# Layer 1 of a two-layer kernel: the third image's angle products placed ahead of the second-half result products of the first image

## The chip, the core and the metric

The kernel runs on one core of a Trainium2 chip. The metric is the device time of one execution in microseconds (us). The kernel before takes 1414.39 us, the median of three runs (1414.35 to 1415.5).

## The reference, cut to what matters

The input is x, 16 images of 128 channels and 64 x 64 places. Layer 0 adds to x a diagonal LSTM over its group-normalised values. Layer 1 adds to that result, again group-normalised, a small quantum circuit at every place; it alone concerns us here.

```python
def L1(x, pre_w, pre_b, q_weights, post_w, post_b):
    xf = x.transpose(0, 2, 3, 1).reshape(-1, C)
    xq = xf @ pre_w.T + pre_b            # four angles for each place
    z = _simulate(xq, q_weights)         # sixteen amplitudes, squared, summed with signs
    out = z @ post_w.T + post_b
    return out.reshape(N, H, W, -1).transpose(0, 3, 1, 2)
...
x = x + L0(_gn(x), ...)
x = x + L1(_gn(x), ...)
```

The kernel writes the product of the starting state as sines of sums of angles, so that an image goes through four steps: angle products, sines, amplitude products with their squares, and result products, to which the bias and the input are added.

## The kernel before, in words

Layer 0 takes most of the time (to about 1283 us) and ends with the statistics of layer 1's normalisation. At its end most of x lies in SBUF: rows 24 to 63 of all images in the tile `ring`, and rows 0 to 23 in DRAM (`low`), from where they come back in pieces of 512 columns.

Layer 1 works image by image, on 8 pieces of 512 columns each: pieces 0 to 2 are the reloaded rows, pieces 3 to 7 lie in `ring`. Images are counted from 0, so the third image is image 2. The helpers are:

- `load(n)` (L948) takes up to n free places and issues as many loads of reloaded rows on GpSimd's queue (L954, the DMA itself at L860).
- `angles(b, c)` (L972) makes eight products (L977) for image b into one PSUM bank, `theta`: four column strips of 32, each the sum of two products. With c = 0 or 1 it takes one half of 256 columns of each piece; without c, all 512. Pool `ps_t` has one bank.
- `sines(b, c)` (L987) is a generator. Its first part reads `theta` on ScalarE (L992, y), rounds on VectorE (L994, near) and subtracts (L995). Its second part, at the next call, is the sine on ScalarE (L997).
- `squares(b, c)` (L999) makes two products of 64 rows each (L1006, am, two banks) and squares them on ScalarE (L1019).
- `outputs(b, h, c)` (L1021) makes four products of 32 rows each (L1028, po) for one half h of the pieces, into four banks of the pool `ps_o`, which has five.
- `finish(b, h, po, c)` (L1038) adds bias and x to each on VectorE (L1053), which frees its bank, and issues the output's DMA on SyncE's queue (L1054). For the reloaded pieces it also gives their places back to `load`.

Each product is recorded as two matmuls. The order is written out by hand (`tc.manual_schedule()`, L1065): each engine executes its instructions in the order of the calls, and the framework only adds the waits. The first image goes in halves of 256 columns, so that work starts early; then image 1 and the rest go whole. From image 1 on, a loop (L1100) repeats: outputs(b, 0), first part of sines(b + 2), finish, load, squares(b + 1), second part of the sines, outputs(b, 1), finish, load, angles(b + 3). Ahead of the loop this pipeline is filled by hand, and there the change lies (L1086 to L1099).

Of the kernel before, what the change touches and what calls it, by code (L numbers as in the profile page):

```python
# [80 lines left out]
def kernel(  # L81
# [866 lines left out]
    def load(n):  # L948

        while n and places and len(lows) < NT * NB:  # L950
            v = places.pop(0)
            lows.append(v)
            if len(lows) > 8:
                low_rows(nc.gpsimd, len(lows) - 1, v)  # L954
            n -= 1

    def rows_of(b, k):
        if k < NT:
            return lows[NT * b + k]
        q = block(2 * ROWS * k)  # L960
        return ring[:, q : q + 2, b, :]

    def half(v, c):

        if c is None:
            return v
        return v[:, c] if len(v.shape) == 3 else v[:, c * BLOCK : (c + 1) * BLOCK]

    def bank(pool, name):
        return pool.tile([P, CHUNK], F32, name=name, tag=pool.name)  # L970

    def angles(b, c=None, all_of=None):  # L972
        th = half(bank(ps_t, f"theta{b}_{c}") if all_of is None else all_of, c)
        for h in range(2):

            for j in (2, 3, 1, 0):
                nc.tensor.matmul(  # L977
                    th[32 * j : 32 * j + 32, :],
                    lhsT=w_image[:, b, 16 - 16 * h : 48 - 16 * h],
                    rhs=half(rows_of(b, 2 * j + h), c),  # L980
                    start=(h == 0),
                    stop=(h == 1),
                    tile_position=(0, 32 * j),
                )
        ths[b, c] = th

    def sines(b, c=None):  # L987

        if b not in turns:
            turns[b] = sinp.tile([P, CHUNK], F32, name=f"y{b}", tag="y")  # L990
        y = half(turns[b], c)
        nc.scalar.activation(y, ths[b, c], AF.Identity, bias=b_image[:, b : b + 1])  # L992
        near = half(nearp.tile([P, CHUNK], F32, name=f"near{b}_{c}", tag="near"), c)
        nc.vector.tensor_scalar(near, y, ROUND, ROUND, ALU.add, ALU.subtract)  # L994
        nc.vector.tensor_sub(y, y, near)  # L995
        yield
        nc.scalar.activation(y, y, AF.Sin, scale=TWO_PI)  # L997

    def squares(b, c=None):  # L999
        ams = []  # L1000
        y = half(turns[b], c)
        for h in range(2):
            am = half(ps_a.tile([P, CHUNK], F32, name=f"am{b}_{h}_{c}", tag=f"am{h}"), c)

            k = 64 * h
            nc.tensor.matmul(  # L1006
                am,
                lhsT=w_amp[k : k + 64, h, :],
                rhs=y[k : k + 64, :],
                start=True,  # L1010
                stop=True,
                tile_position=(k, 0),
            )
            ams.append(am)

        if b not in sqs:
            sqs[b] = [sqp.tile([P, CHUNK], F32, name=f"sq{b}", tag="sq"), turns[b]]
        for am, v in zip(ams, sqs[b]):
            nc.scalar.activation(half(v, c), am, AF.Square)  # L1019

    def outputs(b, h, c=None):  # L1021
        po = [
            half(bank(ps_o, f"po{b}_{h}_{j}_{c}"), c)
            for j in range(4)
        ]
        for j in range(4):
            k = 32 * j
            nc.tensor.matmul(  # L1028
                po[j],
                lhsT=w_out[k : k + 32, :],  # L1030
                rhs=half(sqs[b][h], c)[k : k + 32, :],
                start=True,
                stop=True,
                tile_position=(k, 0),
            )
        return po

    def finish(b, h, po, c=None):  # L1038
        for j in range(4):
            k = 4 * h + j  # L1040
            v = rows_of(b, k)
            x1, y, o = half(v, c), po[j], ov[b, :, k * CHUNK : (k + 1) * CHUNK]
            to = place = v
            if c is not None:
                o, to = o[:, c * BLOCK : (c + 1) * BLOCK], x1
            elif k >= NT:


                q = block(2 * ROWS * k)
                to = ring[:, q, b - 1 : b + 1, :] if b % 2 else ring[:, q + 1, b - 2 : b, :]  # L1050
                y = y.rearrange("p (k n) -> p k n", n=BLOCK)
                place = to.rearrange("p k n -> p (k n)")
            nc.vector.scalar_tensor_tensor(to, y, b_out, x1, ALU.add, ALU.add)  # L1053
            nc.sync.dma_start(out=o, in_=to if c is not None else place)  # L1054
            if c is None or c == 1 and k < NT:
                places.append(place)

    def idle():

        ps = bank(ps_t, nc.get_next_instruction_name())  # L1060
        v = w_image.rearrange("p b k -> p (b k)")[:, 0:CHUNK]
        for _ in range(2):
            nc.tensor.matmul(ps, lhsT=w_out, rhs=v, start=True, stop=True)  # L1063

    with tc.manual_schedule():  # L1065
        load(len(places))

        angles(0, 0)
        angles(0, 1, bank(ps_o, "theta0"))
        first = [sines(0, c) for c in range(2)]  # L1070
        for later in first:
            next(later)

        th = bank(ps_t, "theta1")
        angles(1, 0, th)
        for later in first:
            next(later, None)
        squares(0, 0)
        angles(1, 1, th)
        ths[1, None] = th  # L1080
        po = outputs(0, 0, 0)
        finish(0, 0, po, 0)
        squares(0, 1)
        later = sines(1)
        next(later)
        po = outputs(0, 1, 0)  # L1086
        finish(0, 1, po, 0)
        next(later, None)
        po = outputs(0, 0, 1)
        finish(0, 0, po, 1)  # L1090
        load(3)
        angles(2)
        later = sines(2)
        next(later)
        po = outputs(0, 1, 1)
        squares(1)
        next(later, None)
        finish(0, 1, po, 1)
        angles(3)  # L1099
        for b in range(1, NB):  # L1100
            po = outputs(b, 0)
            later = sines(b + 2) if b + 2 < NB else iter(())
            finish(b, 0, po)
            load(3)
            next(later, None)
            if b + 1 < NB:
                squares(b + 1)
            next(later, None)
            po = outputs(b, 1)
            finish(b, 1, po)  # L1110
            load(3)
            if b + 3 < NB:
                angles(b + 3)
            elif b < NB - 1:
                idle()
# [37 lines left out]
```

## Time and profile before

| | |
|---|---|
| median of three runs | 1414.39 us |
| profiled execution | 1416.6 us |
| its span | 1414.8 us |
| start of layer 1's first angle products | 1288.34 us |
| first output DMA issued | 1294.66 us |
| last result on VectorE | 1401.2 us |
| TensorE busy | 1351.9 us (96%) |
| VectorE busy | 981.1 us (69%) |
| ScalarE busy | 778.4 us (55%) |
| GpSimd busy | 921.3 us (65%) |

The profile is that of one execution. Its times are in us from the start of the span. A row of the timeline gives the start, the length, the engine, the line and the operation with its output, inputs and shapes; xN says that N like instructions are merged. What stands in brackets is the idle time of the engine just ahead, and what ended it. PE is TensorE, DVE is VectorE, ACT is ScalarE, POOL is GpSimd and SPq is SyncE's DMA queue. [...] A row of the table of stretches gives the stretch, then the busy time of each engine in it, the granted share of TensorE's clock, the mean busy share of the 16 DMA engines, and what they moved in GB/s. A share over 1 comes of packets that overlap.

### The profile page before, as it was taken

To read this page: it belongs to the slowest core of one execution; us is meant where nothing else is said; L and a number is where in the kernel's file an instruction comes from. 1 tells how busy PE (TensorE), PEld (TensorE's weight loads), DVE (VectorE), ACT (ScalarE), POOL (GpSimd) and SP (SyncE) were. 2 spreads that over 40 slices of the span, in tenths; PEclk is the share of its full clock that TensorE was granted. 3 is DMA by queue.
4 is the path that set the end of the run, shared out by engine and by line. 5 is a ranking of instruction groups with operands and counts; after the bars stand their busy time and mean duration, and the time that the engine had idled before them with its cause. 6 is when DMAs were issued, how large, how long until landed. Compare 5 with 4: busy or idle time off the path is not lost. (4 is left out here: it accounts for less than half of the span.)

```text
span 1414.8 us, 20302 instructions
## 1 busy us (share of the span) xinstructions
PE 1351.9 (96%) x6030; PEld 960.6 (68%) x6030; DVE 981.1 (69%) x2549; ACT 778.4 (55%) x1860; POOL 921.3 (65%) x1823
## 2 busy tenths in 40 slices
PE   6778999999999999999999999999999999989995
PEld 5658887777776667667777767677777778785331
DVE  7983565566665666787777776666665567866995
ACT  4555666555555555555555555555555566554331
POOL 4226787777776667788888876777777667762300
PEclk9999999999999999999999999999999999999998
DMA  9980000000000000133333100000000000004999
GB/s 327 368 282 2 1 2 0 1 1 1 1 0 1 0 1 1 60 119 120 119 120 120 60 1 1 0 1 1 1 1 0 1 1 1 9 24 157 371 399 353
DMA packets 78926, 107.06 MB, mean 76 GB/s; under 512 B 5552, under 2 KB 53712, under 8 KB 78816
## 3 DMA queue, kind: packets, MB, share of 16 engines
q1 hardware_dynamic: 74176, 94.39, 19.1%
q0 software_dynamic: 3408, 10.58, 2.1%
q8 instruction: 48, 0.79, 0.2%
q10 hardware_dynamic: 1232, 0.80, 0.2%
q14 instruction: 62, 0.51, 0.1%
HBM read 59.61 MB, written 46.14 MB: 75 GB/s over the span
## 5 line engine op out<-in xcount | busy, mean ns | idle before, releaser
L583 PE MATMUL ps<-spare,wxT 128*128 128x512 f32 (+18 forms) x1280 | 479.7, 518 | 0.7 <-POOL spare L574 0.7
L767 DVE TENSOR_TENSOR ps<-ps,both 128x256 f32<-128x256 f32 (+9 forms) x544 | 221.7, 408 | 304.9 <-PE ps L752 303.4
L771 ACT ACTIVATE ps<-ps,bias 128x512 f32<-128x512 f32 (+23 forms) x480 | 279.3, 583 | 220.2 <-DVE ps L767 183.7
L752 PE MATMUL ps<-spare,w1T 128*128 128x256 f32 (+16 forms) x1272 | 345.8, 353 | 9.8 <-DVE spare L834 4.9
L583 PEld LDWEIGHTS ps<-spare,wxT 128*128 128x128 f32 x1280 | 230.9, 190 | 173.2 <-issue 155.5
L752 PE MATMUL ps<-spare,w0T 128*128 128x256 f32 (+16 forms) x1272 | 343.8, 352 | 0.8 <-POOL spare L608 0.8
L802 ACT COPY both<-ps 128x256 f32<-128x256 f32 (+9 forms) x544 | 191.6, 355 | 180.8 <-PE ps L752 161.2
L617 POOL TENSOR_TENSOR ring<-ring,spare 128x256 f32<-128x256 f32 (+8 forms) x487 | 247.7, 541 | 31.2 <-DVE stats L705 21.1
L752 PEld LDWEIGHTS ps<-spare,w1T 128*128 128x128 f32 x1272 | 229.8, 190 | 35.7 <-DVE spare L834 7.6
L752 PEld LDWEIGHTS ps<-spare,wsT 128*128 128x128 f32 x1088 | 194.9, 190 | 86.4 <-DVE spare L834 34.7
L752 PE MATMUL ps<-spare,wsT 128*128 128x256 f32 (+14 forms) x1088 | 241.3, 365 | 5.4 <-DVE spare L834 3.6
L752 PEld LDWEIGHTS ps<-spare,w0T 128*128 128x128 f32 x1272 | 230.3, 190 | 22.1 <-POOL spare L608 0.9
L574 POOL TENSOR_TENSOR spare<-spare,rstd 128x512 f32<-128x512 f32 (+10 forms) x160 | 171.1, 1069 | 14.8 <-DVE rstd L153 2.3
L569 POOL TENSOR_TENSOR spare<-ring 128x256 f32<-128x256 f32 (+8 forms) x213 | 147.6, 703 | 0.0
L828 ACT ACTIVATE g<-cst 128x256 f32<-128x256 f32 (+20 forms) x320 | 103.0, 368 | 64.4 <-DVE cst L827 63.8
L564 POOL TENSOR_TENSOR spare<-ring,mean 128x16 f32<-128x16 f32 (+8 forms) x247 | 131.2, 541 | 7.4 <-DVE mean L143 7.2
L834 DVE TENSOR_TENSOR spare<-g,ps 128x256 f32<-128x256 f32 (+17 forms) x319 | 105.4, 368 | 43.9 <-ACT g L828 42.0
L608 POOL TENSOR_TENSOR spare<-spare 128x240 f32<-128x240 f32 (+9 forms) x136 | 102.7, 755 | 29.6 <-DVE spare L834 25.7
L771 ACT ACTIVATE g<-ps,bias 128x512 f32<-128x512 f32 (+20 forms) x160 | 97.4, 609 | 27.1 <-DVE ps L767 21.1
L827 DVE TENSOR_TENSOR cst<-cst,ps 128x256 f32<-128x256 f32 (+20 forms) x320 | 104.5, 368 | 5.5
L854 POOL COPY spare<-spare 128x16 f32<-128x16 f32 x64 | 21.1, 330 | 133.8 <-DVE spare L834 133.8
L824 DVE TENSOR_TENSOR ps<-ps,g 128x512 f32<-128x512 f32 (+20 forms) x160 | 95.1, 594 | 17.0 <-ACT g L771 16.6
(368 smaller groups left out, 1096.6 us busy)
## 6 DMA issues: line engine op xcount, KB each, us to landing
out_dram<-ring SPq DMA_DIRECT2D x94, 256.0 KB, 5.1
ring<-in_x_dram SPq DMA_DIRECT2D x80, 256.0 KB, 5.6
low<-ring SPq DMA_DIRECT2D x6, 2048.0 KB, 7.5
ring<-in_x_dram SPq DMA_DIRECT2D x6, 2048.0 KB, 8.1
spare<-in_x_dram SPq DMA_DIRECT2D x27, 256.0 KB, 5.5
rest<-in_x_dram SPq DMA_DIRECT2D x21, 256.0 KB, 5.6
ring<-low POOLq DMA_DIRECT2D x19, 256.0 KB, 6.3
out_dram<-spare SPq DMA_DIRECT2D x14, 256.0 KB, 6.5
```

The lines of the kernel that those rows point to most:

```text
L564: nc.gpsimd.tensor_sub(by_pairs(xn, 0, j, n), x0, over(mean1, n))
L569: nc.gpsimd.tensor_sub(by_pairs(xn, 1, j, n), lower, of)
L574: nc.gpsimd.tensor_mul(v, v, r)
L583: nc.tensor.matmul(ps[g][:, :, a:b], lhsT=wxT[:, g * 128 : (g + 1) * 128], rhs=xns[t % 2][:, :, a:b], start=t > 0, stop=True, skip_group_c ...
L617: engine.tensor_add(x1, x1, by_pairs(new, q, j, n))
L752: nc.tensor.matmul(out, lhsT=w[:, g * 128 : (g + 1) * 128], rhs=rhs, start=False, stop=True, skip_group_check=True,)
L767: nc.vector.tensor_add(v, v, both[g][:, a:b])
L771: nc.scalar.activation(to[:, :, a:w], ps[g][:, :, a:w], FUNC[g], bias=bias[:, g : g + 1])
L802: nc.scalar.copy(both[g][:, a:b], ps[g][:, 0, a:b])
L827: nc.vector.tensor_add(c[:, q], c[:, q], ig[:, q])
L828: nc.scalar.activation(th[:, q, a:w], c[:, q], AF.Tanh)
L834: nc.vector.tensor_mul(new[:, q, a:v], th[:, q, a:v], act[GO][:, q, a:v])
```

## The change

The call angles(2) moves up by three calls. It stood behind outputs(0, 0, 1), its finish and load(3); it now stands ahead of all three, right behind the second part of image 1's sines.

```diff
         po = outputs(0, 1, 0)
         finish(0, 1, po, 0)
         next(later, None)
+        angles(2)
         po = outputs(0, 0, 1)
         finish(0, 0, po, 1)
         load(3)
-        angles(2)
         later = sines(2)
         next(later)
         po = outputs(0, 1, 1)
```

In the built program only TensorE's order differs: the eight products of L977 for image 2 stand ahead of the four of L1028 for outputs(0, 0, 1). The instructions of VectorE, ScalarE, GpSimd and SyncE stand in the same order as before.

## The prediction

> **What bounds the kernel now.** I read the page first, then the chain of waits, then the timeline of layer 1 around the edit, then the busy time by stretch. The chain runs through TensorE products for nearly all of layer 1, but it names the engine that the others wait beside, so I looked at VectorE (DVE) in the timeline. Columns: start, length, engine and line, operation.
>
> ```profile
> 1296.06 0.43 DVE L994 TENSOR_SCALAR near_None<-y 128x512 f32<-128x512 f32 x1 [0.25 <-ACT y L992]
> 1297.12 1.65 DVE L1053 SCALAR_TENSOR_TENSOR ring<-po,b_out,ring 128x256 f32<-128x256 f32 x4
> 1298.69 1.26 DVE L1053 SCALAR_TENSOR_TENSOR spare<-po,b_out,spare 128x256 f32<-128x256 f32 x3
> 1299.87 0.48 DVE L1053 SCALAR_TENSOR_TENSOR ring<-po,b_out,ring 128x256 f32<-128x256 f32 x1
> 1303.48 0.43 DVE L994 TENSOR_SCALAR near_None<-y 128x512 f32<-128x512 f32 x1 [3.13 <-ACT y L992]
> 1304.55 1.65 DVE L1053 SCALAR_TENSOR_TENSOR ring<-po,b_out,ring 128x256 f32<-128x256 f32 x4
> 1307.33 2.07 DVE L1053 SCALAR_TENSOR_TENSOR spare<-po_None,b_out,spare 128x512 f32<-128x512 f32 x3 [1.13 <-PE po_None L1028]
> ```
>
> DVE is idle 3.13 us from 1300.35 to 1303.48, because ScalarE had no angles of the third image (image 2) to read, and 1.13 us before 1307.33. After that it has no gap: in the stretch table below it is busy 82.83 of 84 us. So the two idle times at the start of layer 1 are what can be won. TensorE and ScalarE in the same stretch:
>
> ```profile
> 1295.33 0.69 ACT L992 ACTIVATE y<-theta,b_image 128x512 f32<-128x512 f32 x1
> 1295.95 0.67 PE L1028 MATMUL po<-sq,w_out 32*128 32x256 f32 x2
> 1297.66 1.48 PE L1028 MATMUL po<-sq,w_out 32*128 32x256 f32 x6 [1.04 <-DVE ring L1053]
> 1299.07 1.03 PE L977 MATMUL theta_None<-ring,w_image 128*32 128x512 f32 x2
> 1302.61 0.71 PE L1028 MATMUL po<-y,w_out 32*128 32x256 f32 x8
> 1303.26 1.13 PE L1006 MATMUL am_None<-y,w_amp 64*128 64x512 f32 x4
> 1306.17 1.14 PE L1028 MATMUL po_None<-sq,w_out 32*128 32x512 f32 x8
> ```
>
> The second-half products outputs(0,0,1) start at 1295.95 with one free bank, stand 1.04 us, and then follow DVE bank by bank (1297.66 to 1299.07). Image 2's angles come behind them: 1299.07 to 1302.61 is 3.54 us, where image 3's take 1.85 (1304.32 to 1306.17). The clock column tells why. Columns by stretch: sum, PE, PEld, DVE, ACT, POOL busy, PEclk, DMA share, GB/s.
>
> ```profile
> 1299.00:1300.00 1.00, 1.00 (x9) 0.30 (x12) 1.00 (x4) 0.00 (x0) 0.00 (x0) 0.58 0.81 268
> 1300.00:1301.00 1.00, 1.00 (x12) 0.31 (x8) 0.35 (x1) 0.00 (x0) 0.00 (x0) 0.50 0.77 264
> 1301.00:1302.00 1.00, 1.00 (x8) 0.00 (x0) 0.00 (x0) 0.00 (x0) 0.21 (x1) 0.50 0.75 262
> 1302.00:1303.00 1.00, 1.00 (x12) 0.31 (x8) 0.00 (x0) 0.24 (x1) 0.99 (x3) 0.72 0.34 114
> ```
>
> The granted clock is half for (0.42+0.50+0.50+0.28)/0.5 = 3.4 us, 1299.15 to 1302.55, right behind the thin stretch of TensorE. The end itself belongs to the DMA engines:
>
> ```profile
> 1296.00:1317.00 21.00, 19.96 (x113) 6.42 (x116) 16.55 (x32) 7.12 (x13) 4.30 (x8) 0.92 0.73 239
> 1317.00:1401.00 84.00, 82.10 (x440) 26.68 (x432) 82.83 (x131) 28.14 (x47) 13.97 (x26) 1.00 1.03 396
> 1401.00:1413.00 12.00, 0.00 (x0) 0.00 (x0) 0.22 (x1) 0.00 (x0) 0.00 (x0) 0.52 0.93 351
> ```
>
> From 1317 they are full (share 1.03), and they drain for 11 to 12 us after DVE's last result at 1401.2. Before 1317 they are at 0.73, so 0.27 x 21 = 5.7 us of them lie idle. A shift in layer 1 reaches the end only by taking DMA idle time out of that stretch.
>
> [...]outputs(0,0,1) restarts at 1297.66, 0.06 us after DVE read a bank (1297.12 + 0.48). [...]
>
> **The change, part by part.** One call moves: on TensorE the eight angle products of image 2 (16 records) go ahead of the four of outputs(0,0,1). Nothing is added or removed. DVE, ACT, POOL and SP keep their orders; load(3) keeps its place in POOL's queue, and no DMA is moved.
>
> - *The new start of angles(2).* Its bank is the single theta bank, free when ScalarE has read image 1's angles: 1295.33 + 0.69 = 1296.02. So it starts at about 1296.1, where before one product of outputs(0,0,1) ran. Behind this wait stand outputs(0,0,1), which could start one product 0.1 us earlier; nobody takes that product before 1298.69. The rows of image 2 were loaded long before: the DMA engines are empty from 1292.3 to 1295. At full clock it takes 1.85, to 1297.95.
> - *outputs(0,0,1).* Its banks come free at 1295.81, 1297.60, 1297.99 and 1298.38. From 1297.95 it runs at the same pace as now, and DVE, occupied until 1298.77, takes it from 1298.69 or 1298.75 on as now. Price 0 to 0.1 us, hidden by DVE's own queue; without that cover it would be 1.85.
> - *outputs(0,1,1)* loses its cover. Now it finds all banks free and takes 0.65 as a set. Then it needs the banks that DVE frees from outputs(0,0,1); the last but one comes at 1299.48 + 0.48 = 1299.96. The fourth product starts at 1300.02 and takes 0.63 alone (as 1298.44 to 1299.07 now), to 1300.65. Without this wait it could end at about 1299.7: the new wait costs 0.95, inside the gain.
> - *squares(1)* then starts at 1300.65 instead of 1303.26: **2.61 us earlier**. Its inputs (sine of image 1, 1297.24 + 0.63 = 1297.87) are there. angles(3) follows 1.06 later at 1301.7 and outputs(1,0) at 1303.56; DVE takes the first full-width result at 1307.33 - 2.61 = 1304.72. Image 2's sines run meanwhile: ScalarE reads the angles at 1298.1, DVE rounds at 1300.35 instead of 1303.48 and finishes outputs(0,1,1) at 1303.1. So one idle of 1.6 us remains, instead of 3.13 and 1.13: 4.26 - 1.65 = 2.61 again.
> - *The clock.* The 2.61 holds 1.7 from the dip (3.4 us at half) and 0.9 of order alone: without the dip now, angles(2) would end 1.7 earlier. That the dip goes is an estimate[...]. If it stays, squares(1) and angles(3) pay about 1.3.
> - *Through the DMA engines.* Outputs from outputs(0,1,1) on are issued 2.6 earlier, into a stretch at 0.73. Only the three loads at 1301.79 stay; they land 3.0 us after issue, so by about 1306, ahead of angles(4) at 1310.51 - 2.6 = 1307.9. I take off 0.1 for their meeting the earlier outputs (0 to 0.5). Full DMA then begins near 1314.4 and ends 2.5 earlier.
>
> Sum: -2.6 + 0.1 = -2.5 against the profiled execution (span 1414.8, 1416.6 in all, 1.8 around the span), giving 1412.3 and 1414.1. The median shown is 2.2 below the profiled execution; I carry the difference over: 1414.39 - 2.5 = **1411.9**.
>
> **Rivals.**
> - *No dip in ordinary runs*[...]: only the 0.9 of order is won: 1413.5. For it: the median is 2.2 below the profiled run.[...]
> - *The dip stays or moves onto squares(1) and angles(3)*: 2.6 - 1.3 = 1.3: 1413.1.
> - *DMA-bound whatever is done*: the tail of 12 us swallows the shift, 1414.4. Against: 5.7 us of DMA idle lie ahead of 1317.
> - *Slower, by a dip that the change makes.* Between 1297.95 and 1300.65 TensorE would have only products of 32 rows paced by DVE. [...]half clock falls on angles(3) and outputs(1,0), which nothing covers: +1.7. It decides where the run before had no dip: -0.9 + 1.7 = +0.8: 1415.2.
> - *More than the sum*: were TensorE ready when DVE is, at 1303.1, all 4.26 us of idle would go; with half of the rest, or longer dips now, 3.5: 1410.9.
>
> **How the numbers follow.** Forecast 0.52 (its own range 1411.2 to 1412.6), no dip 0.14, dip stays 0.09, hidden in DMA 0.06, slower 0.08, more 0.11. 0.2% is 2.8 us, about what a measurement can tell from no change, and the bound of faster is 1411.6. Faster: 0.11 and a fifth of the forecast, 0.22. Slower by that much: half of the slower case, 0.04. The rest, 0.74, is within 0.2%. The range 1411.0 to 1413.8 leaves out hidden, slower and half of more, 0.2.
>
> **What would show it.** Right: the theta products of image 2 at 1296.1 taking 1.85; no half clock near 1300; DVE's idle of 3.13 gone and one of about 1.6 before outputs(1,0); DMA full by 1314. Wrong: outputs(0,0,1) later than 1298.8 at DVE, half clock at 1301 to 1305, or a DVE end at 1398.6 with the DMA end still at 1413.

## The result and the profile after

The changed kernel takes 1412.94 us (median of 21 runs, 1412.08 to 1415.7) and the kernel before 1415.5 (21 runs, 1413.18 to 1417.05): 2.56 us less, a ratio of 0.9982 with a 95% interval of 0.9976 to 0.9988. In us the interval is about 1.7 to 3.4. The profiled execution took 1412.49, its span 1410.7. Two later comparisons gave 0.9979 (0.9970 to 0.9989) and 0.9979 (0.9971 to 0.9987), 3.2 and 2.8 us less. The median of three runs that stands ahead of the prediction, 1414.39, was 1.1 us under that of the 21 runs.

VectorE in the timeline of the changed kernel. Layer 1 starts 0.36 us earlier in this execution (first result of `finish` at 1293.78 instead of 1294.14), so 0.36 is to be added to each time before it is laid beside those of the kernel before.

```profile
1295.69 0.43 DVE L994 TENSOR_SCALAR near_None<-y 128x512 f32<-128x512 f32 x1 [0.25 <-ACT y L992]
1296.76 1.65 DVE L1053 SCALAR_TENSOR_TENSOR ring<-po,b_out,ring 128x256 f32<-128x256 f32 x4
1298.33 1.26 DVE L1053 SCALAR_TENSOR_TENSOR spare<-po,b_out,spare 128x256 f32<-128x256 f32 x3
1299.51 0.48 DVE L1053 SCALAR_TENSOR_TENSOR ring<-po,b_out,ring 128x256 f32<-128x256 f32 x1
1299.90 0.42 DVE L994 TENSOR_SCALAR near_None<-y 128x512 f32<-128x512 f32 x1
1300.96 1.65 DVE L1053 SCALAR_TENSOR_TENSOR ring<-po,b_out,ring 128x256 f32<-128x256 f32 x4
1304.34 2.07 DVE L1053 SCALAR_TENSOR_TENSOR spare<-po_None,b_out,spare 128x512 f32<-128x512 f32 x3 [1.73 <-PE po_None L1028]
```

The rounding of image 2 follows the last result without a wait; the idle time of 3.13 us is gone. The one ahead of the full-width results has grown from 1.13 to 1.73. Counted from the first `finish`, VectorE reaches those results at 1304.34 - 1293.78 = 10.56 us, where it was 1307.33 - 1294.14 = 13.19: 2.63 earlier. TensorE and ScalarE:

```profile
1294.97 0.69 ACT L992 ACTIVATE y<-theta,b_image 128x512 f32<-128x512 f32 x1
1295.72 0.62 PE L977 MATMUL theta_None<-ring,w_image 128*32 128x512 f32 x2
1297.58 1.20 PE L1028 MATMUL po<-sq,w_out 32*128 32x256 f32 x8
1298.47 1.87 PE L1028 MATMUL po<-y,w_out 32*128 32x256 f32 x8
1300.27 1.13 PE L1006 MATMUL am_None<-y,w_amp 64*128 64x512 f32 x4
1303.18 1.14 PE L1028 MATMUL po_None<-sq,w_out 32*128 32x512 f32 x8
```

The angles start as soon as ScalarE has left the theta bank (1294.97 + 0.69 = 1295.66) and take 1.86 us. outputs(0,1,1) now takes 1.87 as a set, bank by bank behind VectorE, where it took 0.71. Matmuls of one set overlap: those of the angles start at 1295.72 and 1296.18 and are 0.62 and 0.60 long. The stretch that ran at half clock before:

```profile
1299.00:1300.00 1.00, 1.00 (x7) 0.74 (x6) 1.00 (x4) 0.00 (x0) 0.00 (x0) 1.00 0.80 264
1300.00:1301.00 1.00, 1.00 (x6) 0.30 (x4) 0.97 (x3) 0.00 (x0) 0.00 (x0) 1.00 0.76 266
1301.00:1302.00 1.00, 1.00 (x10) 0.29 (x12) 1.00 (x4) 0.57 (x2) 0.56 (x2) 1.00 0.76 260
1302.00:1303.00 1.00, 1.00 (x12) 0.13 (x4) 0.61 (x2) 1.00 (x3) 0.99 (x2) 1.00 0.74 155
```

The clock column reads 1.00 throughout. TensorE's busy time is 1.00 in each of these rows, as it was in the kernel before at a clock of 0.50 to 0.72: a busy TensorE is not one at its peak. And the DMA engines (last two columns):

```profile
1296.00:1317.00 21.00, 20.86 (x128) 7.04 (x124) 19.13 (x36) 7.72 (x13) 5.89 (x11) 1.00 0.85 289
1317.00:1401.00 84.00, 80.19 (x424) 26.22 (x424) 80.20 (x127) 27.51 (x46) 12.57 (x23) 0.99 1.04 400
1401.00:1413.00 12.00, 0.00 (x0) 0.00 (x0) 0.00 (x0) 0.00 (x0) 0.00 (x0) 0.51 0.58 221
```

Ahead of 1317 their share rose from 0.73 to 0.85, so 0.12 x 21 = 2.5 us of their idle time is gone there, and less is left for the last stretch (0.58 x 12 = 7.0 us of work where it was 0.93 x 12 = 11.2). One thing was not foreseen. TensorE in the timeline at angles(5), and VectorE behind it:

```profile
1313.84 1.05 PE L977 MATMUL theta_None<-ring,w_image 128*32 128x512 f32 x4
1315.03 0.62 PE L977 MATMUL theta_None<-spare,w_image 128*32 128x512 f32 x2
...
1318.03 2.07 DVE L1053 SCALAR_TENSOR_TENSOR low<-po_None,b_out,low 128x512 f32<-128x512 f32 x3 [0.94 <-PE po_None L1028]
```

The angles of image 5 wait for their third reloaded piece, 1.04 us in the timeline (DMA spare<-low), and VectorE stands 0.94 us. Of the 2.63 that VectorE won, it gives this back in this profile. The second profile of the changed kernel, described below, has no such wait, and its layer 1 is no shorter.

### The profile page after: what moved, and what is told of

The parts are those of the page before. It is cut to its first block, busy times and chain, and to the rows that moved or that the text cites. A ratio compares the mean times of both kernels' runs of the same rounds, so it can differ in the third digit from the quotient of the medians.

```text
span 1410.7 us, 20301 instructions
## 1 busy us (share of the span) xinstructions
PE 1352.7 (96%) x6030; PEld 962.4 (68%) x6030; DVE 980.5 (70%) x2549; ACT 778.7 (55%) x1860; POOL 921.3 (65%) x1823
```

## The experiments

The theory: the gain is made of 1.7 us of half clock and 0.9 of order at VectorE, and it reaches the end because it takes idle time from the DMA engines. Rivals: the order alone, the clock alone, VectorE rather than the DMA engines at the end. Since the first result of `finish` stands anywhere from 1293.50 to 1295.54 in profiles with the same layer 0, the table counts layer 1 by itself: from the first result of `finish` (L1053) to the first full-width one, and to the end of the span. A difference of 0.4 there is within what three profiles of one kernel show. The time is the median of the runs of that kernel, and the ratio is to the kernel before in the same comparison, whose median was 1415.5 to 1416.35.

| kernel | time | ratio, 95% | to first full-width result | to the end |
|---|---|---|---|---|
| before (two profiles) | 1415.5, again 1415.86 | | 13.19, 13.16 | 120.7, 119.8 |
| changed (three profiles) | 1412.94, 1413.09, 1413.10 | 0.9982, 0.9979, 0.9979 | 10.56, 10.56, 10.57 | 116.9, 117.0, 117.3 |
| before, with filler | 1414.26 | 0.9989 (0.9983 to 0.9996) | 11.49 | 118.1 |
| changed, squares(1) moved | 1412.42 | 0.9974 (0.9965 to 0.9984) | 9.63 | 117.4 |
| changed, no output of image 8 | 1408.03 | 0.9942 (0.9927 to 0.9958) | 10.56 | 112.0 |
| one step further | 1416.59 | 1.0003 (0.9994 to 1.0011) | 15.29 | 121.8 |
| one step further, with filler | 1414.87 | 0.9992 (0.9986 to 0.9999) | 12.24 | 118.8 |
| changed, seven places, first placing | 1414.95 | 0.9989 (0.9983 to 0.9996) | 10.56 | 116.7 |
| changed, seven places, own pool | 1414.78 | 0.9992 (0.9986 to 0.9999) | 10.56 | 116.3 |
| squares(1) moved and seven places | 1413.86 | 0.9986 (0.9979 to 0.9994) | 9.64 | 115.4 |

**The changed kernel again, and the kernel before again.**

> The changed kernel once more, to have it beside the others on one chip. Theory (order and clock): about 2.5 us under the median of the kernel before, with the granted clock of nearly all runs at 0.995 or 0.996; the runs of the kernel before fall into two groups, one near 1413.6 at the higher clock and one near 1416.6 at the lower. Rival (order alone): the groups of the kernel before are noise and have nothing to do with the clock.

1413.09 (10 runs) beside 1416.27 (34 runs). The granted clock of the changed kernel's runs was 0.994 to 0.996, that of the kernel before 0.991 to 0.995. There are no two clean groups: the runs of the kernel before lie all over 1413.7 to 1417.8, one at 1419.6. The mean clock goes roughly with the time: of the runs of the kernel before, the nine at 0.992 have a median of 1416.5, the three at 0.993 of 1417.2, the 18 at 0.994 of 1415.4, the three at 0.995 of 1414.4. But this profile of the changed kernel also starts the scan of layer 0 at 105.3 us, where the first one has 103.9, and reaches layer 1 1.8 us later (1295.54 instead of 1293.78). So the spread comes in part from layer 0, and what I said of two groups falls. VectorE has no wait at angles(5) in this profile: the load for it is issued 15.75 us after the first `finish` (1311.29 - 1295.54), where it was 16.46 (1310.24 - 1293.78). VectorE's last result comes 104.5 us after the first `finish` instead of 105.5, and layer 1 still takes 117.0, as with the wait (116.9 and, in the third profile, 117.3).

> The kernel before once more, for a second profile of it. Theory: a half-clock stretch[...] somewhere between 1298 and 1304[...]; DMA engines at 399 to 405 GB/s in the full stretch as in the other profiles, so that the 400 against 405 of the first pair was chance. Rival: 400 again, a lower rate that belongs to the old order.

The second profile of the kernel before has the same wait in the timeline,

```profile
1303.28 0.43 DVE L994 TENSOR_SCALAR near_None<-y 128x512 f32<-128x512 f32 x1 [3.13 <-ACT y L992]
```

and half clock again, for 3.4 us from 1298.9 to 1302.3 (worked out from a granted clock of 0.91 in the 6 us to 1299.95 and 0.71 in the 4 us behind them). Two profiles with one such stretch each do not show how often it comes. The DMA engines moved 405 GB/s in the 60 us from 1319.95, where the first profile shows 400 in the same place and the changed kernel 405. So the lower rate does not belong to the old order. Over 60 us it makes 0.75 us, and the earlier layer 0 of the changed kernel 0.36: together most of the 1.5 by which the first pair of profiles (4.1 us apart) differs more than the medians (2.6).

**Filler in place of the angles.**

```diff
         next(later, None)
+        warm_up(2)    # two products of 128x512 into the bank am0, which nobody reads
         po = outputs(0, 0, 1)
```

> The kernel before, in its own order, with two filler products of 128x512 put ahead of outputs(0,0,1), where the change puts the angles of image 2. They take as long at full clock (1.7 us), and write a bank that nobody reads. Theory (order and clock): no half clock near 1300, angles(2) in 1.85 instead of 3.54 us, VectorE's idle time before image 2's rounding 3.13 - 1.7 = 1.4 us; the time is that of the kernel before in its runs without a dip, 1413.6, so 1.5 to 3 under its median, and still about 1 over the changed kernel. Rival (order alone): no gain over the kernel before, since the angles still come behind outputs(0,0,1). Rival (clock alone): as fast as the changed kernel, 1412.6.

The clock stayed at 1.00 from 1288 to 1320, and VectorE's two waits in the timeline became

```profile
1301.82 0.43 DVE L994 TENSOR_SCALAR near_None<-y 128x512 f32<-128x512 f32 x1 [1.41 <-ACT y L992]
...
1305.65 2.07 DVE L1053 SCALAR_TENSOR_TENSOR spare<-po_None,b_out,spare 128x512 f32<-128x512 f32 x3 [1.11 <-PE po_None L1028]
```

3.13 became 1.41, and the other wait stayed (1.13 and 1.11). Image 2's rounding, which waits for angles(2), comes 7.66 us after the first `finish` (1301.82 - 1294.16) instead of 9.34 (1303.48 - 1294.14), 1.68 earlier. The half clock therefore costs 13.19 - 11.49 = 1.70 at VectorE, and the order 11.49 - 10.56 = 0.93. In time, 2.0 of the 3.2 us are won by work that computes nothing, so order alone falls. The other 1.2, from this kernel to the changed one, is not settled by the medians, whose intervals overlap; that clock alone falls too is read from VectorE's 0.93 and from layer 1, 118.1 against 116.9 to 117.3.

The granted clocks of all runs agree with a dip in ordinary runs of the kernel before, as an estimate. Their mean is 0.9934 for the kernel before (34 runs), 0.9945 with the filler (21) and 0.9950 for the changed kernel (10). Half clock for 3.4 us takes 1.7 / 1414 = 0.0012 from the mean of one run, and the filler gave back 0.0011.

**squares(1) moved as well.**

```diff
-        po = outputs(0, 1, 1)
         squares(1)
+        po = outputs(0, 1, 1)
```

> The changed kernel, with squares(1) also moved, ahead of outputs(0,1,1). TensorE stands between the banks of outputs(0,1,1) there, so the 1.06 us of squares(1) should fit into that wait; angles(3) then starts 1.0 earlier. Theory: VectorE's idle time before the full-width results falls from 1.73 to about 0.7, and the end comes 0.5 to 1.0 earlier than the changed kernel, as far as the DMA engines still have idle time before 1304 (0.26 of 4 us). Rival (the DMA engines are full from the first full-width outputs on whatever is done): VectorE gains its 1.0, the end gains less than 0.3.

```profile
1303.13 2.07 DVE L1053 SCALAR_TENSOR_TENSOR spare<-po_None,b_out,spare 128x512 f32<-128x512 f32 x3 [0.81 <-PE po_None L1028]
```

VectorE gained 0.93 there, as expected, and lost more later; the only other wait of its timeline ahead of the last image is

```profile
1318.63 2.07 DVE L1053 SCALAR_TENSOR_TENSOR low<-po_None,b_out,low 128x512 f32<-128x512 f32 x3 [2.74 <-PE po_None L1028]
```

on a product that waited for reloaded pieces. Layer 1 takes 117.4, no less than the changed kernel's 116.9 to 117.3, where 0.5 to 1.0 less was expected. By the median it is 0.67 faster than the changed kernel on the same chip, with intervals that overlap (0.9974 and 0.9979 to before); it has the lowest median of the kernels that write the whole result, but its lead over the changed kernel is not settled.

**The end without 2.1 MB of output.**

```diff
-            nc.sync.dma_start(out=o, in_=to if c is not None else place)
+            if b != 8:
+                nc.sync.dma_start(out=o, in_=to if c is not None else place)
```

> The changed kernel without the eight output DMAs of image 8, 2.1 MB; all else is computed as before, so that image's output is not written. Theory (the end belongs to the DMA engines, at about 400 GB/s from 1304 on): the end comes 2.1 MB / 400 GB/s = 5.2 us earlier, while VectorE's last result stays within 0.5 us of 1399. Rival (VectorE, busy without a gap, sets the end): the end moves less than 1 us.

Layer 1 takes 112.0 instead of 117.1 (the mean of three), 5.1 less, and the median is 5.1 under the changed kernel's 1413.1. VectorE's last results in the timeline of this run:

```profile
1394.56 5.36 DVE L1053 SCALAR_TENSOR_TENSOR ring<-po_None,b_out,ring 128x512 f32<-128x512 f32 x8 [0.76 <-PE po_None L1028]
```

They end at 1399.9, 104.9 after the first `finish`; in the changed kernel it is 1393.94 + 5.36 - 1293.78 = 105.5. The end moved by the bytes, 5.1 us where 5.2 was expected, and VectorE by 0.6. The end belongs to the DMA engines.

**One step further.**

```diff
         next(later)
+        angles(2)
         po = outputs(0, 1, 0)
         finish(0, 1, po, 0)
         next(later, None)
-        angles(2)
```

> The change pushed one step further: angles(2) ahead of outputs(0,1,0) too. Theory: the single theta bank is read by ScalarE until 1296.0 whatever the order, so outputs(0,1,0) now waits for that and for 1.85 us of angles, ends about 1298.6, and VectorE waits 1.5 us between its rounding and finish(0,1,0). All that follows is 1.5 later than in the changed kernel: about 1.2 to 1.5 us slower than that, still 1.5 to 2 faster than the kernel before. Rival (the earlier the angles the better): as fast as the changed kernel or faster.

It was expected 1.5 to 2 us faster than the kernel before, and is as slow (1416.59 beside 1416.35). The foreseen wait came, 1.45 us; and one that was not expected here, 4.92:

```profile
1298.82 1.66 DVE L1053 SCALAR_TENSOR_TENSOR ring<-po,b_out,ring 128x256 f32<-128x256 f32 x4 [1.45 <-PE po L1028]
...
1309.59 0.75 DVE L1053 SCALAR_TENSOR_TENSOR spare<-po_None,b_out,spare 128x512 f32<-128x512 f32 x1 [4.92 <-PE po_None L1028]
```

The stretches of the same run show why (PE busy is the second number, PEclk the third from the end):

```profile
1298.20:1301.60 3.40, 3.25 (x21) 2.32 (x22) 2.78 (x8) 0.69 (x1) 0.00 (x0) 1.00 0.35 115
1301.60:1305.00 3.40, 3.40 (x13) 1.15 (x15) 3.04 (x8) 0.04 (x1) 1.49 (x3) 0.50 0.73 238
1305.00:1308.40 3.40, 3.40 (x16) 0.45 (x13) 0.00 (x0) 1.56 (x3) 0.12 (x1) 0.50 0.83 271
```

The thin stretch of 32-row products is now behind the angles, 4.8 us of it (1298.09 to 1302.85), and two stretches of 3.40 us at half clock follow, on squares(1) and angles(3), which nothing covers. This is the prediction's slower rival, one call beyond the change. With one filler product ahead of outputs(0,0,1) and one ahead of outputs(0,1,1):

> The order that was pushed one step too far, with one filler product of 128x512 ahead of outputs(0,0,1) and one ahead of outputs(0,1,1), in waits for banks. Theory (the two windows at half clock came from the thin stretch behind angles(2), 1298.1 to 1302.8): full clock throughout, VectorE's idle time before the full-width results 4.92 falls to between 1.2 and 2, the wait of 1.45 ahead of finish(0,1,0) stays, and the time is about 1.5 over the changed kernel, 1414.6. Rival (the order itself costs the time): as slow as without fillers.

```profile
1306.33 2.07 DVE L1053 SCALAR_TENSOR_TENSOR spare<-po_None,b_out,spare 128x512 f32<-128x512 f32 x3 [1.73 <-PE po_None L1028]
```

4.92 falls to 1.73, as in the changed kernel, the wait of 1.45 for the theta bank stays, and the kernel is 1.8 slower than the changed one beside it (1413.10), where 1.5 was expected: the order costs that. VectorE reaches the full-width results 3.05 earlier (12.24 instead of 15.29), most of the 3.4 that 6.8 us at half clock take (an estimate from the rows above); so the rest is put down to the clock.

**A seventh place for reloaded rows.** The two tiles of constants `w_theta` and `wide_sb` were put with layer 0's tiles, which made room for one more tile.

```diff
-    places = list(spare) + [lowp.tile([P, CHUNK], F32, name=f"low{i}") for i in range(6)]
+    places = list(spare) + [lowp.tile([P, CHUNK], F32, name=f"low{i}") for i in range(7)]
```

> The changed kernel with one more place for reloaded rows (seven instead of six; room is made by putting two tiles of constants with layer 0's). One load of 256 KB moves from the full stretch into the empty one ahead of the first outputs. Theory (DMA idle time is what counts): 0.26 MB / 400 GB/s = 0.65 us earlier than the changed kernel. The wait of angles(5) for its rows (1.19 us) goes or moves to a later image. Rival (VectorE and its waits set the end): the time follows VectorE's last result, not the DMA engines.

This run does not answer its question. Placed in one pool with the statistics, the tiles made the first loads wait for layer 1's first products: in GpSimd's timeline three of them stand at 1291.58, behind a wait of 5.68 us (PE theta), where the changed kernel issues six at 1284.19. And layer 0 reached its scan 2 us later, at 105.96 instead of 103.94. The second placing, in a pool of its own:

> The changed kernel with a seventh place for reloaded rows again, the two tiles of constants this time in a pool of their own, so that the first loads do not wait for layer 1's first products. Theory (DMA idle time is what counts): the first seven loads run ahead of the first output, 0.26 MB leaves the full stretch, and layer 1 from its first finish to the end takes 0.65 us less than the 116.9 us of the changed kernel. The time is 0.6 under the changed kernel on the same chip, unless layer 0 starts its scan later, as it did with the other placing (first product at 105.96 instead of 103.9 to 104.3). Rival (waits for loads at VectorE set the end): layer 1 unchanged at 116.9.

Layer 1 takes 116.3, against 116.9, 117.0 and 117.3: 0.6 to 1.0 less in this one profile, where 0.65 was expected. VectorE's wait of 0.94 is gone from its timeline, which by itself shows nothing of the seventh place, since the changed kernel also has a profile without it. Layer 0 is lengthened again: the first `finish` stands at 1296.72 in this profile; why, was not tried. So the kernel as a whole is slower than the changed one.

> The changed kernel with squares(1) ahead of outputs(0,1,1) and with the seventh place. Theory: both take DMA idle time away, 0.5 and 0.65 us; about 1.1 under the changed kernel on the same chip if layer 0 is not lengthened. Rival: only one of them counts, since loads and outputs fill the same idle time: 0.6.

Both together bring layer 1 to 115.4, the shortest, 1.6 under the mean of the changed kernel, where 1.1 was expected; the wait of 2.74 that the moved squares(1) had run into is gone from this profile. Layer 0 took it back: 1413.86.

> The changed kernel beside the others on this chip: 2.5 to 3.2 us under the kernel before.

1413.10 (14 runs), 2.8 under the 1415.90 of the kernel before (62 runs).

## Why the prediction was right, step by step

- *Start and length of angles(2).* Foreseen 0.08 behind ScalarE's read, 1.85 long; measured 0.06 and 1.86.
- *outputs(0,0,1).* VectorE took it without a gap, as foreseen.
- *outputs(0,1,1).* The new wait for banks was priced at 0.95 and an end at 1300.65, which is 1300.29 on the clock of the changed profile; squares(1) started at 1300.27.
- *2.61 us at VectorE.* Measured 2.63, and split by the filler into 1.70 and 0.93 for the 1.7 and 0.9 of the sum. This is where the mechanism is shown.
- *The clock.* The dip went: the clock reads 1.00 from 1294 to 1317 in the first profile of the changed kernel and from 1288 to 1320 in the second, and the third reaches the full-width results in the same time (10.57). Why it should go was the author's estimate. The rival of a dip that stays falls. The rival of no dip in ordinary runs falls too, as far as profiles and averages can tell: both profiles of the kernel before have one, filler won 2.0 us in the medians, and it raised the mean granted clock by what one dip takes, 0.0011 against 0.0012.
- *Through the DMA engines.* The sum allowed 2.5 at the end; the medians say 2.56, 3.2 and 2.8, and layer 1 by itself 120.2 - 117.1 = 3.1. Whether the term was a little small is open, since single profiles lie up to 0.9 apart (120.7 and 119.8) and the first interval is 1.7 to 3.4; so is the 0.1 taken off for loads that meet the earlier outputs. That the first median agrees with the forecast to 0.06 is luck. Full DMA was foreseen near 1314.4, and from 1313.8 on the share is 1.0 or more. It was not foreseen that it would be so already from 1304.8 to 1311.8 (0.89 to 1.08), with two us at 0.75 between.
- *The absolute time.* 1411.9 was forecast and 1412.94 measured. The 1.0 lies in the starting point, 1414.39 from three runs, and not in the difference. The measured 0.18% is on the inner side of the 0.2% of which the prediction speaks, and the two later comparisons, 0.21%, on the outer: on which side it fell is chance.
- *The step that failed* is in the DMA term: "Only the three loads at 1301.79 stay", checked against angles(4) alone. Angles(4) had time. The load for angles(5) hardly moved either. It was issued at 1311.22 before and landed 3.3 us later, 2.3 ahead of angles(5) at 1316.84. In the changed kernel angles(5) could start 2.6 earlier, but the load was issued only 0.6 earlier (0.98 in the trace, less the 0.36 of layer 0), and landed 4.7 after its issue. It needs a place that an output of image 1 must leave first, and these outputs took 4.5 us to land instead of 2.6 (medians), with the DMA engines full from 1304.8 on. It cost VectorE 0.94 of its 2.63 in two of three profiles, and nothing at the end: the profile without this wait has the same layer 1.
- *The slower rival* did not come with the change, but with the same call one place higher. In the changed kernel 1.86 us of products of all 128 rows stand in the middle of the thin stretch instead of ahead of it, and 2.7 us are left thin behind them (1297.58 to 1300.27); one step further it is 4.8, and 6.8 us at half clock follow in the one profile of it. The changed kernel shows no dip there, in the profiles named above.

## What to carry to other kernels

Where an engine is paced by the release of banks, look for work that needs none of those banks and put it into that wait. Here VectorE took the delayed products without a gap, and the clock stayed at 1.00 where it had been half for 3.4 us. Look at what is left thin behind the moved work: one call further, the clock stood at 0.50 for 6.8 us behind it. And find out what ends last. In this kernel the DMA engines are full nearly to the end (share 1.01 from 1401 to 1405, 0.74 to 1409), and VectorE's last result could come 1.0 us earlier without moving the end; what counted was the idle time of those engines that the earlier outputs removed.

## What the runs showed of the hardware that was not expected

TensorE's busy time did not tell where the clock would fall. Ahead of the dip of the kernel before (1295.7 to 1299.1) it was busy 2.36 of 3.40 us, with no gap over 1.04. In the run one step further it was busy 3.25 of the 3.40 us ahead of the half clock (1298.2 to 1301.6). Both stretches hold products of 32 rows that waited for banks. With 1.86 us of products of all 128 rows within such a stretch (the changed kernel), or two filler products of 128x512, the clock stayed at 1.00. Whether the rows in use decide it, or the waits, no run here tells apart.

Moving two small tiles of constants in SBUF to make room for one more place, with the code of layer 0 unchanged, went with a longer layer 0. In the first profile of it the scan starts at 105.96 us, where six profiles without it show 103.7 to 105.3; the first `finish` stands at 1295.88, 1296.72 and 1295.96 in the three profiles of it, at 1293.50 to 1295.54 in the ten others. The cause stays open.
